# A four-layer graph network on one core: the beginning rewritten, half-block places split, the end taken by quarters

## The chip, the cores and the metric

The kernel runs on one core of a Trainium2 chip. TensorE (PE) multiplies and transposes, VectorE (DVE) and ScalarE (ACT) do the element-wise work, GpSimd (POOL) takes a little of it, and SyncE (SP) issues nearly all transfers between DRAM and the on-chip memory. The metric is the device time of one execution in microseconds (us); the time of the kernel before is the median of three runs, 4793.08 us (4787.59 to 4794.63).

## The reference, cut to what matters

Eight graphs (batches) of 2048 nodes with 128 features share one 0/1 adjacency matrix of 2048 x 2048. Four layers follow each other, each of the form `x = x + layer(relu(layernorm(x)))`:

```python
def layer0(x):                       # graph attention, one head
    x = x * node_weights[None, :, None] + node_bias[None, :, None] + x
    h = layernorm(x @ W) * ln_gamma + ln_beta
    s1, s2 = h @ a1, h @ a2
    e = leaky_relu(s1[:, :, None] + s2[:, None, :], 0.2)
    att = softmax(where(adj > 0, e, NEG_INF))
    return elu(att @ h + h)
def layer1(x):                       # attention with 4 heads of 32
    scores = where(adj == 0, -inf, q @ k.T / sqrt(32))
    return softmax(scores) @ v @ W_o + b_o
def layer2(x):                       # mean over the neighbours
    agg = (mask @ x) / maximum(deg, 1.0)
    return relu(x @ W_self + b_self + agg @ W_neigh + b_neigh)
def layer3(x):                       # graph attention, one head, no norm inside
    h = x @ W.T
    e = leaky_relu(s[:, :, None] + d[:, None, :], 0.2)
    return softmax(where(adj == 0, -1e9, e)) @ h
```

## The kernel before

**Units.** A row tile is 128 nodes (16 of them, `T`), a quarter is four row tiles (512 nodes, `G` = 4 quarters). Layers 0 and 3 work in six groups of destination tiles, `GROUPS`: four of three tiles and two of two (`n` = 3 or 2).

**Masks.** At the start each of the 16 row tiles of `adj` is loaded (1 MB, L1144) and turned into 0/1 in bf16 (`nb01`, VectorE, L1146). ScalarE makes of it an int8 mask (`pmt`, L1149; stored to DRAM as `pm_all`, L1152; the sum of the row is the degree's source). PE transposes the tile in 16 pieces into two PSUM tiles (`pmask`, L1162); VectorE copies the first (L1165), ScalarE the second (L1167) into `mst`, an fp8 mask, stored per group as `mg_all` (L1169). From that the fp8 tiles of layer 2, `mt_all`, are copied in DRAM (L1206, `regroup`). `degrees` makes the reciprocal degrees.

**Layers 0 and 3** (`gat_loop`). `layer0_ahead` makes layer 0's input: `weigh`, `scale` and `shift` on POOL (L592, L618, L621), two norms, transposes (`ptr`, L379), products (`ph`, L393). The node scores of one side are laid along the free dimension of all partitions by way of DRAM: `along_free` (row, `rowd`, broadcast load). `gat_rows` does that for all nodes (`s2b`, 1 MB); `gat_maximum` (L445) finds for one destination tile the greatest score among its neighbours with one VectorE pass over 128x2048; the maxima and scores of a group go the same way into `ab`. Then, for each of eight steps of a group, two source tiles at a time: `leaky` (ScalarE, L508), `lowered` (subtract the maximum, VectorE, L514), `exps` (ScalarE, L518), `masked` (VectorE, L523), `product` (PE, L534, into `gacc`), each stage one step behind the former; `finish` writes the result.

**Layer 1.** `before_attention` makes `q`, `k` and `v` of a batch, quarter by quarter, stores them and loads them back in the layouts that attention reads. The attention itself is 256 blocks (batch, 256 destination rows, head), each of 12 sub-steps: two halves (128 rows each) of six. In a half-block PE makes `sc` (S, L932), VectorE masks it and takes its maximum (`ttr`, L948, two of 128x1024, maxima in `amh`, `amn`), ScalarE takes exponentials (`exp`, L956), and PE transposes the result of a block before in two tiles `pt` (T0, T1, L968), which ScalarE copies to `eT` (C0, C1, L973), for the products with the values (V, `acc`, L983). Before: T0 at sub-step 3, T1 and C0 at 4, C1 at 5. At the end of a block's pair of heads `finished` transposes and normalises (`po`, `aoT`), and `back` multiplies with W_o (`pwo`, L1041) and adds to `x` (L1046); its functions are called one per sub-step from `pending`.

**Layer 2.** `layer2` makes the input (`pre2`: norm, `hm` in two bf16 parts, `h2T`), then for each quarter of destinations the sum over neighbours (`agg`: 48 matmuls `pagg`, L787, on `mt` tiles that `fetch` loads), scales it (`agT`, L805) and combines (`pn`, `y`).

**PSUM.** `psum(...)` gives one of three buffers. Results in it are read late: `later(f)` queues the reader, `settle` runs all of them, and `psum` runs the oldest when no buffer is free.

**The order.** Under `manual_schedule` the written order of PE, ScalarE, VectorE and POOL instructions is the order of their queues; SP's transfers are placed by the framework. The program is written in three stretches. First, `run(rest)`: ten masks merged with layer 0's input of batch 0, its row, its loop with six more masks, `before_attention(0)`. Second, the main periods, one for each batch: `work(side, end)` calls attention's sub-steps (`mains`) and after each a share of the side work by weights (layers 2 and 3 of the batch before, layer 0 of the next); `locked` puts one loop step per three sub-steps, each function of it into one of three cells by `PLACES` (or `PLACES_B` in the second half of a half-block), so that it stands at a fixed place among attention's instructions. In the last period the side work is layers 2 and 3 of batch 6. Third, the tail: `pre2`, `agg` with `pre3` partly between, and `loop3` of batch 7.

Of the kernel before, what the change touches and what calls it, by code (L numbers as in the profile page):

```python
# [31 lines left out]
def gnn_kernel(  # L32
# [167 lines left out]
    wq = load_w("wq", W_q)  # L200
    wk = load_w("wk", W_k)
    wv = load_w("wv", W_v)
    wo = load_w("wo", W_o)
    wself = load_w("wself", W_self)
    wneigh = load_w("wneigh", W_neigh)
    w3 = load_w("w3", W3)
    gam = load_row("gam", ln_g)
    bet = load_row("bet", ln_b)
    bo1 = load_row("bo1", b_o)
    bself = load_row("bself", b_self)  # L210
    bneigh = load_row("bneigh", b_neigh)

    nc.vector.tensor_scalar(bo1, bo1, -1.0, None, ALU.add)
# [28 lines left out]
    ones = const.tile([P, P], F32, name="ones")  # L242
# [5 lines left out]
    w0T = const.tile([P, P], F32, name="w0T")  # L248
# [7 lines left out]
    pw3 = psum("pw3", (P, P))  # L256
    nc.tensor.transpose(pw3, w3, ident)
    nc.vector.tensor_copy(w3T[:, 0:P], pw3)

    pwa = psum("pwa", (P, 2))  # L260
    nc.tensor.matmul(pwa, w3, a12_3, start=True, stop=True)
    nc.vector.tensor_copy(w3T[:, P : P + 2], pwa)
# [133 lines left out]
    def along_free(col, dst, n):  # L396
# [5 lines left out]
        for g in range(4):  # L402
            nc.sync.dma_start(
                out=d[0:n, g * 32 : (g + 1) * 32], in_=row[g * 32 : g * 32 + n, :]
            )
# [27 lines left out]
    def gat_rows(st):  # L433

        st["s2b"] = new(sp2, "s2b", "s2b", (P, N))
        along_free(st["s2n"], st["s2b"], T)
# [12 lines left out]
    def gat_loop(st, finish, maxima, gap):  # L449
# [15 lines left out]
        def maximum(k, q):  # L465
            i0, n = GROUPS[k]
            if maxima and q < n:
                gat_maximum(st, i0 + q)
# [4 lines left out]
        def shifts(k):  # L473
# [3 lines left out]
            nc.vector.tensor_tensor(u, s1, st["mn"][:, i0 : i0 + n], ALU.subtract)  # L477
# [5 lines left out]
        def spread(k):  # L483
            n = GROUPS[k][1]
            t = new(abp, "ab", "ab", (P, 2 * n * P))
            along_free(gr[k]["cab"], t, 2 * n)
# [94 lines left out]
    def layer0_ahead(b):  # L581
# [3 lines left out]
        def load(g):  # L585
            h[g] = new(hp3, "h", "h", (P, 4, P))
            nc.sync.dma_start(out=h[g], in_=x_chunk(b, g))

        def weigh(g):
            for k in range(4):  # L590
                t = 4 * g + k
                nc.gpsimd.tensor_scalar(  # L592
# [24 lines left out]
        def scale(g):  # L617
            nc.gpsimd.tensor_tensor(hv(g), hv(g), bc_mid(gam, 4), ALU.mult)  # L618

        def shift(g):  # L620
            nc.gpsimd.tensor_tensor(hv(g), hv(g), bc_mid(bet, 4), ALU.add)  # L621
# [52 lines left out]
    attn, ready = {}, {}  # L674

    def before_attention(b):
# [34 lines left out]
        def project_v(g):  # L711
# [16 lines left out]
        steps = Steps()  # L728
        steps.skewed(
            G,  # L730
            norm_stages(lambda g: xb[g], hdst) + [turned, project, project_v],
            1.0,
        )
        return steps

    def layer2(b):
# [26 lines left out]
        def rest1(g):  # L763
# [6 lines left out]
        steps = Steps()  # L770
        steps.skewed(
            G,
            norm_stages(lambda g: xb[g], hdst) + [part0, rest0, part1, rest1],
            4.0,
        )
# [63 lines left out]
        return steps, agg  # L839

    def layer3(b, gap=1):
# [13 lines left out]
        def project(g):  # L855
            if g == 0:
                st["haug"] = new(bp, "big", "haug", (P, T, P + 1))
# [9 lines left out]
        pre = Steps()  # L867
        pre.skewed(
            G,
            norm_stages(lambda g: xb[g], hdst)  # L870
            + [turned, project],
            1.0,
        )
        pre.add(0.5, settle)
        pre.add(1.0, lambda: gat_rows(st))
# [16 lines left out]
        return pre, gat_loop(st, finish, True, gap)  # L892
# [99 lines left out]
    def finished(blk):  # L992
# [45 lines left out]
        def back():  # L1038
# [7 lines left out]
            ao["last"] = later(lambda: nc.vector.tensor_tensor(xg, pw, xg, ALU.add))  # L1046
# [12 lines left out]
    SUB = 12  # L1059
    state = {"exp": None, "old": None, "older": None, "ahead": None, "pair": None, "ao": None}  # L1060

    def block_steps(n):
# [36 lines left out]

        def sub(t, s):  # L1100
            def go():
                if t == 0 and s == 0:
                    begin()
                old, older = state["old"], state["older"]
                if s == 0 and n < len(blocks):
# [294 lines left out]
```

## Time and profile before

| What | Value |
|---|---|
| median of 3 runs | 4793.08 us (4787.59 to 4794.63) |
| the profiled execution | 4792.7 us |
| its span | 4790.8 us |
| instructions | 87729 |
| mean granted TensorE clock | 0.943 |
| PE, DVE, ACT, POOL busy | 4126.7, 3906.3, 3613.4, 454.9 us |
| first mask (`nb01`) starts | 14.3 us |
| first step of layer 0's loop | 117.7 us |
| first exponential of attention | 296.9 us |
| last attention update of `x` | 4572.2 us |

The page cuts the span into 40 slices of 119.8 us; a digit is the busy share of a slice in tenths. Stages can be asked for by windows. A line of the timeline gives start, length, engine, line of the kernel, operation, written and read tile with shapes, and in brackets the engine's idle time before it and what ended it. Busy times are of one profiled execution; the time of that execution is the span and 1.9 us around it.

### The profile page before, as it was taken

How to read it: one execution, taken by the hardware profiler on the slowest of the kernel's cores; microseconds unless marked ns; L12 is line 12 of the kernel's file. 1: busy time of each engine (PE TensorE's matmuls, PEld its weight loads, DVE VectorE, ACT ScalarE, POOL GpSimd, SP SyncE). 2: the span in 40 equal slices, each digit the busy share in tenths (PEclk: the TensorE clock that was granted, in tenths of full speed). 3: DMA queues.
4: the chain of work that ended last, by engine and by line, in shares of the span. 5: the costliest groups of instructions: out<-in, count | busy, mean ns of one | idle time of the engine just before them, and what ended most of it. 6: DMA issues, size and time to landing. Idle time of an engine off the chain costs nothing.

```text
span 4790.8 us, 87729 instructions
## 1 busy us (share of the span) xinstructions
PE 4126.7 (86%) x33290; PEld 2842.0 (59%) x33290; DVE 3906.3 (82%) x8337; ACT 3613.4 (75%) x5121; POOL 454.9 (9%) x413
## 2 busy tenths in 40 slices
PE   2569998998898988998799988989889998989976
PEld 2535665576656666575665766567665666646645
DVE  5967777888978898788988889788987898658849
ACT  4637986698868988598885978689885988749926
POOL 2020002001200031001300012000310000000000
PEclk7768999999999999999999999999999999999988
DMA  8432113323232232412233132322324123222122
GB/s 268 137 91 57 46 40 114 95 59 102 79 123 62 68 103 76 133 51 86 82 103 102 59 101 77 120 66 68 103 74 134 50 73 99 79 77 61 52 89 76
DMA packets 308354, 423.34 MB, mean 88 GB/s; under 512 B 61222, under 2 KB 177628, under 8 KB 303836
## 3 DMA queue, kind: packets, MB, share of 16 engines
q1 hardware_dynamic: 305984, 416.85, 28.7%
q8 instruction: 263, 4.31, 0.4%
q14 instruction: 159, 1.30, 0.1%
q10 hardware_dynamic: 1948, 0.87, 0.1%
HBM read 365.78 MB, written 55.98 MB: 88 GB/s over the span
## 4 chain that ended last, share of the span: by engine, by line
PE 33%; DVE 29%; ACT 28%; issue 6%; DMA 3%; SPq 1%; ACTq 0%; DVEq 0%
ACT e L956 8%; ACT eT L973 8%; PE pt L968 7%; DVE e L948 7%; PE pagg L787 7%; PE gacc L534 6%; ACT ge L508 6%; PE sc L932 5%; DVE dump L445 4%; DVE ge L514 4%; DVE ge L523 4%; PE acc L983 3%; ACT ge L518 3%; PE ph L393 1%; DVE ln_s L336 1%
## 5 line engine op out<-in xcount | busy, mean ns | idle before, releaser
L973 ACT COPY eT<-pt 128x1024 f32<-128x1024 f32 x1024 | 1007.3, 1012 | 568.7 <-PE pt L968 566.0
L948 DVE CUSTOM_DVE_ANT_0 e<-sc,pm 128x1024 f32<-128x1024 f32 x1024 | 1211.5, 1220 | 212.0 <-PE sc L932 207.0
L534 PE MATMUL gacc<-haug,ge 128*128 128x129 f32 x8192 | 1122.4, 288 | 178.3 <-DVE ge L523 94.6
L968 PE MATMUL pt<-ident,e 128*128 128x128 f32 x8192 | 1079.0, 282 | 159.0 <-DVE amh L948 74.1
L534 PEld LDWEIGHTS gacc<-haug,ge 128*128 128x128 f32 x8192 | 1016.7, 199 | 335.5 <-issue 264.8
L968 PEld LDWEIGHTS pt<-ident,e 128*128 128x128 f32 x8192 | 943.5, 145 | 285.1 <-DVE amh L948 101.7
L956 ACT ACTIVATE e<-e,amn 128x2048 f32<-128x2048 f32 x512 | 1031.4, 2014 | 29.6 <-DVE amn L952 29.6
L508 ACT ACTIVATE ge<-ab,s 128x384 f32<-128x384 f32 (+1 forms) x1536 | 803.5, 577 | 121.5 <-DMA ab<-rowd 74.0
L932 PE MATMUL sc<-ks,qr 32*128 32x512 f32 x4096 | 786.9, 660 | 71.5 <-ACT eT L973 46.2
L514 DVE TENSOR_TENSOR ge<-ge,ab 128x768 f32<-128x768 f32 (+1 forms) x768 | 683.8, 890 | 52.5 <-ACT ge L508 46.2
L523 DVE SCALAR_TENSOR_TENSOR ge<-mg,ge 128x768 f32<-128x768 fp8e4 (+1 forms) x768 | 666.6, 868 | 24.7 <-ACT ge L518 23.2
L518 ACT ACTIVATE ge<-ge 128x768 f32<-128x768 f32 (+1 forms) x768 | 595.1, 776 | 118.0 <-DVE ge L514 115.9
L445 DVE CUSTOM_DVE_ANT_0 dump<-s2b,pmg 128x2048 bf16<-128x2048 f32 x256 | 585.5, 2287 | 39.4 <-DMA s2b<-rowd 32.2
L983 PE MATMUL acc<-eT,vv 128*32 128x256 f32 x8192 | 587.6, 397 | 2.6 <-ACT eT L973 2.6
L346 POOL TENSOR_TENSOR ln_r<-ln_ve,neg_half 128x4 f32<-128x4 f32 x160 | 207.2, 1295 | 3868.4 <-DVE ln_ve L340 3623.7
L983 PEld LDWEIGHTS acc<-eT,vv 128*32 128x32 f32 x8192 | 206.8, 111 | 508.7 <-issue 428.0
L932 PEld LDWEIGHTS sc<-ks,qr 32*128 32x128 f32 x4096 | 241.6, 189 | 263.9 <-ACT eT L973 142.5
L787 PE MATMUL pagg<-mt,hm 128*128 128x512 fp8e4 x1536 | 356.1, 381 | 9.3 <-DVE agT L805 9.3
L787 PEld LDWEIGHTS <-hm 128*128 128x128 bf16 x1536 | 147.2, 98 | 183.6 <-issue 30.7
L379 PE MATMUL ptr<-ident,h 128*128 128x128 f32 x512 | 92.3, 307 | 54.2 <-DVE amh L948 19.3
L1036 DVE TENSOR_TENSOR aoT<-po,rT 128x256 f32<-128x256 f32 x64 | 27.1, 424 | 127.6 <-ACT rT L1031 127.5
L379 PEld LDWEIGHTS ptr<-ident,h 128*128 128x128 f32 x512 | 66.8, 155 | 85.5 <-issue 28.8
(126 smaller groups left out, 2601.8 us busy)
## 6 DMA issues: line engine op xcount, KB each, us to landing
pmg<-pm_all SPq DMA_DIRECT2D x256, 256.0 KB
mg<-mg_all SPq DMA_DIRECT2D x128, 384.0 KB
pm<-pm_all SPq DMA_DIRECT2D x128, 256.0 KB
qr<-qd SPq DMA_DIRECT2D x1024, 32.0 KB
mt<-mt_all SPq DMA_DIRECT2D x64, 512.0 KB
ab<-rowd SPq DMA_DIRECT2D x64, 384.0 KB
adj<-in_adj_dram SPq DMA_DIRECT2D x16, 1024.0 KB
s2b<-rowd SPq DMA_DIRECT2D x16, 1024.0 KB
```

The costliest lines, as they stand in the source:

```text
L445: nc.vector.tensor_tensor_reduce(dump, st["s2b"], pm, UP, HIGHEST, ALU.add, ALU.min, st["mn"][:, it : it + 1])
L508: nc.scalar.activation(e[:, c, :], gr[k]["s1"], AF.Prelu, bias=st["s2"][:, j : j + 1], alpha=ALPHA)
L514: nc.vector.tensor_tensor(e, e, bc_mid(gr[k]["m"], 2), ALU.subtract)
L523: nc.vector.scalar_tensor_tensor(e, mt, BIG, e, ALU.mult, ALU.min)
L534: nc.tensor.matmul(gr[k]["acc"][:, q, :], e[:, c, q * P : (q + 1) * P], st["haug"][:, j, :], start=(j == 0 and q == 0), stop=(j == T - 1), ...
L787: nc.tensor.matmul(st["pa"], st["hm"][:, j, s, :], st["mt", g, j // 8][:, j % 8, :], start=(j == 0 and s == 0), stop=(j == T - 1 and s == ...
L932: nc.tensor.matmul(blk["sc"][g // 2][:, (g % 2) * 512 : (g % 2 + 1) * 512], blk["q"][r, t * P : (t + 1) * P], ks_t[b, hh][r, :], start=Tru ...
L948: nc.vector.tensor_tensor_reduce(e[:, c], blk["sc"][h], pm[:, c], UP, HIGHEST, ALU.add, ALU.min, mh[:, h : h + 1])
L956: nc.scalar.activation(blk["e"][t], blk["e"][t], AF.Exp, scale=-1.0, bias=blk["mn"][:, t : t + 1], accum_out=blk["ao"]["sum"][:, t, blk["h ...
L968: nc.tensor.transpose(pt[:, c, t, :], blk["e"][t][:, j * P : (j + 1) * P], ident)
L973: nc.scalar.copy(eT, blk.pop(("pt", w)).rearrange("p c t n -> p c (t n)"))
L983: nc.tensor.matmul(pair["acc"][g * HD : (g + 1) * HD, blk["hh"] % 2, :], vv_t[blk["b"], blk["hh"]][:, j, :], blk["eT"][w][:, g, :], start= ...
```

## The change

**The beginning.** Ten constants that layer 0 doesn't need are loaded from SP after the first inputs, and what is derived from them is made later. The inputs `h` and four tiles of `adj` are loaded ahead. `weigh`, `scale` and `shift` of batch 0 run on VectorE. `nb01` comes from a pool of two buffers, all 16 transposes of a mask go to one PSUM tile that ScalarE copies alone, and a mask's work is in three skewed stages. Eleven masks are merged with layer 0's input; the other five stand before or in the first steps of the loop. Three of the four quarters of `before_attention(0)` are put into layer 0's loop, after the groups that end them.

**Half-blocks.** Places are counted in six sub-steps, given by `ORDER`: T0 and T1 both at 3, C0 at 4, C1 at 5. `locked` has six cells for a loop step, of which every second is preceded by a sub-step; the side work's share is 0.55 for 0.6.

**The end.** In the last main period, after layer 3 of batch 6, stand layer 2's input of three quarters of batch 7 and the first seven entries of `agg` (one load, six gathers: 36 matmuls). In the tail layer 3's input is written by quarters between the gathers, the row `s2b` in two halves, and the maxima by halves of 1024 (32 instead of 16); the first halves stand among the gathers. The mask tiles for them are loaded four at a time.

```diff
-    w3 = load_w("w3", W3)
...
-    nc.vector.tensor_scalar(bo1, bo1, -1.0, None, ALU.add)
+    late = [("wq", W_q), ("wk", W_k), ("wv", W_v), ("wo", W_o), ("wself", W_self)]
...
+    def load_late():
+        for t, ap in late.values():
+            nc.sync.dma_start(out=t, in_=ap if len(ap.shape) == 2 else ap.partition_broadcast(P))
...
-                gat_maximum(st, i0 + q)
+                if "halves" in st:
+                    st["halves"][2](1, i0 + q)
+                else:
+                    gat_maximum(st, i0 + q)
...
-            nc.vector.tensor_tensor(u, s1, st["mn"][:, i0 : i0 + n], ALU.subtract)
+            if "halves" in st:
+                mnh = st["mnh"][:, :, i0 : i0 + n]
+                nc.vector.tensor_tensor(u, mnh[:, 0, :], mnh[:, 1, :], ALU.min)
+                nc.vector.tensor_tensor(u, s1, u, ALU.subtract)
+            else:
+                nc.vector.tensor_tensor(u, s1, st["mn"][:, i0 : i0 + n], ALU.subtract)
...
-    def layer0_ahead(b):
+    def layer0_ahead(b, eng=nc.gpsimd):
...
-            nc.gpsimd.tensor_tensor(hv(g), hv(g), bc_mid(gam, 4), ALU.mult)
+            eng.tensor_tensor(hv(g), hv(g), bc_mid(gam, 4), ALU.mult)
...
+        def some(gs):
+            steps = Steps()
+            steps.skewed(
+                len(gs),
+                [
+                    lambda i, f=f: f(gs[i])
+                    for f in norm_stages(lambda g: xb[g], hdst) + [turned, project, project_v]
+                ],
+                1.0,
+            )
...
+        def masks_of(k):
+            t = st["pm", k] = new(ep, "e", "pmh", (P, 4, N), I8)
+            for i in range(4):
+                nc.sync.dma_start(out=t[:, i, :], in_=pm_all[4 * k + i])
+        def rows(half):
+            if half == 0:
+                st["s2b"] = new(sp2, "s2b", "s2b", (P, N))
+                st["mnh"] = small("mnh", (P, 2, T))
+            c = slice(half * 1024, (half + 1) * 1024)
+            along_free(st["s2n"], st["s2b"][:, c], 8 * half, 8)
+        def maximum(half, it):
+            c = slice(half * 1024, (half + 1) * 1024)
+            dump = new(op, "dump", "dump", (P, 1024), BF16)
+            nc.vector.tensor_tensor_reduce(
+                dump, st["s2b"][:, c], st["pm", it // 4][:, it % 4, c], UP, HIGHEST, ALU.add,
+                ALU.min, st["mnh"][:, half, it : it + 1],
+            )
+        stages = norm_stages(lambda g: xb[g], hdst) + [turned, project]
+        if last:
+            st["halves"] = (masks_of, rows, maximum)
+            pre = [Steps([(1.0, [lambda f=f, g=g: f(g)]) for f in stages]) for g in range(G)]
+        else:
+            pre = Steps()
+            pre.skewed(G, stages, 1.0)
+            pre.add(0.5, settle)
+            pre.add(1.0, lambda: gat_rows(st))
...
+            def add():
+                nc.vector.tensor_tensor(xg, pw, xg, ALU.add)
+                summed.append((b, ib // 2))
+            ao["last"] = later(add)
...
+    ORDER = [
+        ["S", "V0", "exp"],
+        ["V1"],
+        ["ttr"],
+        ["T0", "T1"],
+        ["C0"],
+        ["C1"],
+    ]
...
                     begin()
+                for name in ORDER[s]:
+                    part(t, name)
                 old, older = state["old"], state["older"]
-                if s == 0 and n < len(blocks):
-                    scores(blk, t)
...
-                if s in (3, 4) and real("old"):
-                    turned(old, 2 * t + s - 3)
-                if s in (4, 5) and real("old"):
-                    copied(old, 2 * t + s - 4)
...
+        nb01[it] = new(tp, "eT", "nb01", (P, N), BF16)
+        nc.vector.tensor_scalar(nb01[it], adj_t.pop(it), 0.0, None, ALU.is_gt)
+        load_adj(it + 4)
...
+        pt = psum("pmask", (P, T, P), BF16)
+        for jt in range(T):
+            nc.tensor.transpose(pt[:, jt, :], nb01[it][:, jt * P : (jt + 1) * P], ident_bf)
+        later(lambda: nc.scalar.copy(mst[gk][:, :, c : c + P], pt, saturate=False))
...
-        def one(it):
...
-                if g == 0:
-                    nc.vector.tensor_copy(dst, pt, saturate=False)
-                else:
-                    nc.scalar.copy(dst, pt, saturate=False)
...
+        steps.skewed(T, [neighbours, turned_raised, mask_stored], 5.0)
...
-        st0, pre = layer0_ahead(0)
...
+        st0, pre = layer0_ahead(0, nc.vector)
+        for g in range(G):
+            st0["load"](g)
+        for it in range(4):
+            load_adj(it)
+        load_late()
         xs[0] = []
-        load_x(0)
         masks_all = mask_steps()
-        early, late = Steps(masks_all[:10]), Steps(masks_all[10:])
-        rest = merged(early, pre)
-        rest.add(1.0, lambda: gat_rows(st0))
-        rest.extend(merged(layer0_loop(0, st0, True), late, 0.35))
-        rest.extend(before_attention(0))
+        n = 11
+        rest = merged(pre, Steps(masks_all[:n]))
+        rest.add(1.0, lambda: gat_rows(st0), lambda: load_x(0))
+        rest.add(1.0, late_constants)
         run(rest)
+        xb0 = xs[0]
+        loop = layer0_loop(0, st0, True)
+        quarters, queue, others = before_attention(0), [], masks_all[n:]
+        start = len(loop) - 9 * len(GROUPS) - 6
+        for _ in range(3):
+            run([others.pop(0)])
+        n_late = len(others)
+        for k, step in enumerate(loop):
+            run([step])
+            if others and (k + 1) * n_late >= 0.1 * len(loop) * (n_late - len(others)):
+                run([others.pop(0)])
+            for g, group in enumerate((1, 2, 3, 5)):
+                if k == start + 9 * group + 13:
+                    queue.extend(quarters([g]))
+            if queue:
+                run([queue.pop(0)])
+        run(others + queue)
...
-        PLACES = {'product': 1, 'masked': 0, 'exps': 1, 'lowered': 0, 'leaky': 1, 'ended': 1, 'closed': 0, 'maxi': 0, 'other': 2}
-        PLACES_B = {'product': 1, 'masked': 0, 'exps': 0, 'lowered': 1, 'leaky': 0, 'ended': 1, 'closed': 1, 'maxi': 1, 'other': 2}
+        PLACES_A = {
+            "product": 5, "masked": 1, "exps": 3, "lowered": 1, "leaky": 3,
+            "ended": 1, "closed": 1, "maxi": 1, "other": 5,
+        }
+        PLACES_B = {
+            "product": 5, "masked": 1, "exps": 1, "lowered": 3, "leaky": 1,
+            "ended": 3, "closed": 3, "maxi": 0, "other": 5,
+        }
...
+                cell = [[] for _ in range(6)]
+                places = PLACES_B if pos[0] % 6 >= 3 else PLACES_A
...
-                    cell[(i * 3) // len(parts)].append(p)
-                for c in cell:
-                    mains[pos[0]]()
-                    pos[0] += 1
+                    cell[2 * ((i * 3) // len(parts)) + 1].append(p)
+                for i, c in enumerate(cell):
+                    if i % 2 == 1:
+                        mains[pos[0]]()
+                        pos[0] += 1
...
-                    locked(both[n:], tail, 0.6)
+                    locked(both[n:], tail, 0.55)
...
+                pre2, agg = layer2(B - 1)
+                side.extend(pre2(range(G - 1)))
+                side.extend(agg[:7])
...
+        pre3, loop3, (masks_of, rows, maximum) = layer3(B - 1, last=True)
+        beside = {}
+        def put(k, *fns):
+            beside.setdefault(k, []).append((1.0, list(fns)))
+        first = list(pre2([G - 1]))
+        for g in range(G - 1):
+            k = 9 * (g + 1) + 3
+            for i, (_, fns) in enumerate(pre3[g]):
+                put(k + 1 + i, *fns)
+            if g == 1:
+                put(k + 7, lambda: rows(0))
+        for k in range(4):
+            put(20 + 3 * k, lambda k=k: masks_of(k))
+        todo = [(lambda it=it: maximum(0, it)) for it in range(T)]
+        rest = Steps(first)
+        def some(n):
+            for _ in range(n):
+                if todo:
+                    rest.add(1.0, todo.pop(0))
+        for k in range(7, len(agg)):
+            rest.append(agg[k])
+            rest.extend(beside.pop(k, []))
+            if k >= 33:
+                some(1)
+        for k in sorted(beside):
+            rest.extend(beside[k])
+            some(1)
+        for _, fns in pre3[G - 1]:
+            rest.add(1.0, *fns)
+            some(1)
+        rest.add(1.0, settle)
+        rest.add(1.0, lambda: rows(1))
+        some(T)
+        run(rest + loop3)
```

## Prediction

> **What bounds the kernel now.** I read the page first (busy time, the slices, the chain), then the busy time by stage, then the order of events at both ends.
>
> ```profile
> PE 4126.7 (86%) x33290; PEld 2842.0 (59%) x33290; DVE 3906.3 (82%) x8337; ACT 3613.4 (75%) x5121; POOL 454.9 (9%) x413
> PE   2569998998898988998799988989889998989976
> ...
> DVE  5967777888978898788988889788987898658849
> ...
> PE 33%; DVE 29%; ACT 28%; issue 6%; DMA 3%; SPq 1%; ACTq 0%; DVEq 0%
> ```
>
> Three engines share the chain, so no single one is the bound. But the first two slices of PE (119.8 us each) stand at 2 and 5, and the last two at 7 and 6: the ends are slack on PE, the middle is not. By stage (columns: stretch, length, busy PE, PEld, DVE, ACT, POOL, granted clock, DMA share, GB/s):
>
> ```profile
> 0.00:120.00 120.00, 30.66 (x249) 26.57 (x249) 64.22 (x167) 49.07 (x66) 31.36 (x46) 0.77 0.81 268
> 120.00:240.00 120.00, 71.77 (x488) 66.47 (x489) 115.07 (x190) 79.25 (x131) 0.00 (x0) 0.79 0.43 137
> 2670.00:2710.00 40.00, 38.73 (x352) 29.84 (x352) 34.21 (x67) 37.90 (x57) 0.00 (x0) 1.00 0.18 51
> 2940.00:2980.00 40.00, 34.65 (x282) 25.71 (x280) 38.90 (x72) 29.93 (x43) 6.80 (x4) 0.90 0.26 74
> 4560.00:4680.00 120.00, 76.33 (x412) 45.10 (x410) 49.38 (x158) 20.56 (x35) 8.50 (x9) 0.78 0.30 95
> 4680.00:4791.00 111.00, 73.94 (x512) 69.66 (x512) 105.00 (x158) 76.71 (x137) 0.00 (x0) 0.85 0.25 77
> ```
>
> Until 120 us no engine is busy for more than 54%: chains and DMA (0.81) set the pace. From 120 to 240 and from 4680 on, VectorE does (115 of 120, 105 of 111). The middle changes between PE (38.73 of 40) and VectorE (38.90 of 40). From 4560 to 4680 again nobody is full. The events that mark the ends (start, length, instruction, in brackets the idle time before it and what ended it):
>
> ```profile
> 97.34 2.29 DVE L445 CUSTOM_DVE_ANT_0 dump<-s2b,pmg 128x2048 bf16<-128x2048 f32 x1 [10.24 <-DMA s2b<-rowd]
> 117.66 2.13 ACT L508 ACTIVATE ge<-ab,s 128x384 f32<-128x384 f32 x4 [5.12 <-DMA ab<-rowd]
> 287.23 1.23 DVE L948 CUSTOM_DVE_ANT_0 e<-sc,pm 128x1024 f32<-128x1024 f32 x1 [11.78 <-PE sc L932]
> 4572.15 0.42 DVE L1046 TENSOR_TENSOR x<-pwo,x 128x256 f32<-128x256 f32 x1 [0.80 <-PE pwo L1041]
> 4634.73 0.69 DVE L805 TENSOR_TENSOR agT<-pagg,dv 128x512 f32<-128x512 f32 x1 [4.07 <-PE pagg L787]
> 4660.33 2.29 DVE L445 CUSTOM_DVE_ANT_0 dump<-s2b,pmg 128x2048 bf16<-128x2048 f32 x1 [7.41 <-DMA s2b<-rowd]
> ```
>
> So: first leaky of layer 0 at 117.7, x ready at 258.5, attention from 287; after the last attention update (4572.2) come layer 2's gathers to 4634.7, layer 3's input, its row in DMA until 4660.3, and its loop.
>
> **Part 1, the beginning.** (a) *Masks.* Each loses VectorE's cast `mst` (1.23) and gets one ScalarE copy of 128x2048. That form is not in the trace; 128x512 takes 0.58 and 128x1024 1.01, so 1.01 + 2 × 0.43 = 1.87. With `pmt` (1.94 from start to next start) a mask costs ScalarE 3.8. All 16 now stand before the loop: 61, plus layer 0's own 16 × 0.41 + 4 × 0.6 + 4 × 0.59 = 11, from about 16 us on: ScalarE is free at 88. VectorE has 16 × 1.22 of `nb01` and less than that again; the second `nb01` buffer hides PE's 16 transposes (1.07 to 1.89) behind ScalarE. The skewed order puts the last `nb01` before the third maximum; that comes near 82, the row of `cab` near 86, and from it to the first leaky the trace has 6.5 (end) to 9.4 (beginning): 94, taken as 95 against 117.7: **−22.7**.
>
> DMA may not allow that. Some 29 MB (adj 16, masks out 8, rows, maxima's masks, x) must move before it. The 268 GB/s at a share of 0.81 make 331 when full, so 88 us: just enough; at the 268 itself, 108, and −10. Against the change speaks a rule of the Trainium skill ("DMA: Bandwidth & Descriptors", Issuing engines are not separate DMA queues): all issuers end on the same 16 engines, so ten constants (0.65 MB) moved from ScalarE's queue to SP's win no bandwidth, only order. By it I book nothing for that move; its row (19 issues on ScalarE before its first work) would have given 2 or 3 us.
>
> (b) *POOL.* Scaling and shifting of layer 0's input go to VectorE. The trace has one POOL operation at 65.33 and a VectorE one at 65.56, which takes 0.17 at 59.12:
>
> ```profile
> 65.33 1.18 POOL L618 TENSOR_TENSOR haug<-haug,gam 128x512 f32<-128x512 f32 x1 [2.25 <-ACT mst L1167]
> 65.56 0.97 DVE L425 TENSOR_TENSOR ln_z<-ln_z,ln_r 128x8 f32<-128x8 f32 x1
> 59.12 0.17 DVE L425 TENSOR_TENSOR ln_z<-ln_z,ln_r 128x8 f32<-128x8 f32 x1
> ```
>
> The skill ("SBUF — State Buffer", Who interferes with whom) says that a VectorE operation with two inputs in SBUF and a reading POOL operation lock each other out for a whole instruction. By the rule all 31 us of POOL could stand against VectorE; by the row some 8 operations lost 0.8 each, 7 in all, about what 8 × 0.69 + 16 × 0.34 = 11 cost VectorE anew. I take the row: nothing, as VectorE has 45% idle there.
>
> (c) *Loop.* 117.7 to 258.5 is 140.8, VectorE-bound. Four masks leave it (4 × 2.45 = 9.8) and the degrees (5.5); three quarters of `before_attention` enter (2.5 each): 133: **−7.8**. (d) *After it* came four quarters, 258.5 to the first full scores at 285.2. One remains: statistics 1.4, power 1.0, apply 1.1, transposes 1.2, copy 0.6, projection 2.1, two copies 1.2, and 5.7 through DRAM as before: 14.3: **−12.4**. The early loads of the next input save its wait of 2.73 (row at 293.86): **−3**. Part 1: **−46**, between −33 (DMA) and −57.
>
> **Part 2, the 512 half-blocks.** Six half-places for three, both transposes together ahead of the copies, `pwo` behind both. Compared engine by engine, ScalarE's and VectorE's written orders hardly differ; PE's `po`, `pwo` and the gathers move past one transpose group. Counts stay. What can be gained is PE's wait for `pwo` (12.8 on `amh`, 6.9 on `eT`); two fifths of it, **−8**. What can be lost: both transposed tiles taken from PSUM at once, half as much again as PE's waits on `eT` (43.6 in 11 times), +20. Queued behind such a wait on PE are `po`, the side work's gathers and the next scores, for which VectorE's masking then waits.
>
> **Part 3, the last period.** Three of four quarters of layer 2's input move into it, with 36 of 192 gathers. Moved work: VectorE 11.6, ScalarE 5.5, PE 12 × 0.14. In 4440 to 4560 PE and ScalarE are busy for 112.9 and 112.4 of 120, so ScalarE's 5.5 are paid: **+5** (2 to 15). The gathers stand behind the last `pwo`; the hole from 4572 to the first gather hides them (uncovered, 36 × 0.2165 = 7.8):
>
> ```profile
> 4583.26 6.99 PE L787 MATMUL pagg<-mt,hm 128*128 128x512 fp8e4 x24
> ```
>
> **Part 4, the tail.** 24 gathers took 6.99, 0.29 each, later 0.2165. After the change 36 × 0.2165 run from 4572.2 to 4580, beside the last quarter's norm (5 us); its transposes 0.7; then 156 × 0.2165 = 33.8, four pauses of 2.6 less one, 7.7, and layer 3's transposes and projections of three quarters, 1.5 each: 4627 for 4634.7: **−8** (at 0.29, −4). Layer 3's input is then one quarter, 14.3 from `agT` to the row's transpose by its rows, where four took 18.0: **−3.7**. The row still takes 7.4; three maxima of 2.37 become three halves of 1.30, less 0.2 for the new minimum: **−3**. In the loop 13 maxima are halved, 13 × 1.07 less six small operations, and VectorE bounds it: **−12.5**. The first halves (16 × 1.30 = 21) lie in VectorE's idle time (49 of 120 busy); uncovered they would cost 21. Their masks are 16 loads of 256 KB on SP, queued among the gathers' own loads: 4 MB at a DMA share of 0.30, hidden; late, they would hold back VectorE's queue, and with it layer 3's last quarter. Part 4: **−27** (−18 to −36).
>
> Sum: −46 − 8 + 5 − 27 = −76 on the profiled execution's 4792.7 (span 4790.8, 1.9 around it), 0.4 below the median: **4717**.
>
> **Rivals.** *DMA and ScalarE keep pacing the beginning* (0.13): the leaky comes no earlier, since all masks precede it; the gains in (c) and (d) stay. For it: 0.81 DMA share, and 256-byte rows in the last two mask stores. Against: between 20 and 60 us 245 to 395 GB/s were moved. 4717 + 22.7 = 4740. *The tail's work comes back* (0.12): the last period pays VectorE's 11.6 and ScalarE's 5.5 in full, and cold PE, +15 for +5, tail −18: 4736. *PSUM binds the middle* (0.10, the other side): with both transposed tiles out, side matmuls wait for the first copy. For it: single waits on `eT` up to 7.3 us. Against: the copies were already PE's releaser, the later transpose now starts only one place earlier. The sum is spent at 84/512 = 0.16 per half-block; at 0.2 it is 102: 4717 + 8 + 102 = 4827. *The middle does not change at all*, since the orders are the same: 4725, inside the likeliest.
>
> **How the numbers follow.** Likeliest, 0.62: 4717, its own range 4690 to 4745. The first two rivals lie within 4730 to 4760; 0.03 for an unnamed larger gain. The PSUM case splits: 0.02 same, 0.08 slower, left outside. Range 4680 to 4760. Faster by over 0.2% (9.6 us, about what this kernel's measurement can tell from no change) 0.90, same 0.02, slower 0.08.
>
> **What would show it.** First leaky at 95 (over 108: DMA), x at 228, first full scores at 242, first `agT` wait gone, the last `agT` 55 after the last attention update, the loop of layer 3 at 103.5 long; the attention's half-blocks at the same 8.3 mean. It is wrong if half-blocks grow by 0.16, if first-half maxima delay layer 3's last quarter on VectorE, or if the last period grows by over 15.

## The result, and the profile after

The changed kernel takes 4715.71 us (median of 4 runs, 4711.7 to 4720.64) against 4793.85 us before (4 runs): a ratio of 0.984, with a 95% interval of 0.9823 to 0.9857. The forecast was 4717, between 4680 and 4760. The sum came out within 2 us, and none of its four terms did: that it came so near was luck. The profiled execution shows it: its span is 4709.9, 80.9 less than before.

The page of the changed kernel (busy time; slices of PE and VectorE; the chain by engine):

```profile
PE 4116.3 (87%) x33290; PEld 2845.2 (60%) x33290; DVE 3879.8 (82%) x8384; ACT 3619.7 (77%) x5121; POOL 471.4 (10%) x389
PE   3769998998899989999899988999889998989976
...
DVE  5967767888978888788988889788887899758758
...
PE 32%; DVE 32%; ACT 24%; issue 6%; DMA 5%; SPq 1%; POOL 0%; ACTq 0%; DVEq 0%; POOLq 0%
```

The first three slices of PE go from 2, 5, 6 to 3, 7, 6, and the last two still stand at 7 and 6. DMA's share of the chain rises from 3% to 5%. By stage (columns as before: stretch, length, busy PE, PEld, DVE, ACT, POOL, clock, DMA share, GB/s):

```profile
0.00:120.00 120.00, 39.23 (x320) 34.12 (x321) 71.30 (x214) 77.29 (x84) 13.21 (x22) 0.67 0.85 296
120.00:240.00 120.00, 86.04 (x530) 77.87 (x530) 115.96 (x214) 82.28 (x151) 23.33 (x6) 0.79 0.56 152
4560.00:4680.00 120.00, 69.26 (x457) 61.42 (x455) 106.35 (x199) 62.58 (x104) 2.85 (x2) 0.77 0.21 63
```

The events that answer to those shown of before (start, length, instruction, idle time before it and what ended it):

```profile
90.01 2.29 DVE L445 CUSTOM_DVE_ANT_0 dump<-s2b,pmg 128x2048 bf16<-128x2048 f32 x1 [14.56 <-DMA pmg<-pm_all]
110.27 2.13 ACT L516 ACTIVATE ge<-ab,s 128x384 f32<-128x384 f32 x4 [9.32 <-DMA ab<-rowd]
257.40 1.23 DVE L996 CUSTOM_DVE_ANT_0 e<-sc,pm 128x1024 f32<-128x1024 f32 x1 [6.82 <-PE sc L980]
4512.11 7.93 PE L814 MATMUL pagg<-mt,hm 128*128 128x512 fp8e4 x36
4512.31 0.42 DVE L1096 TENSOR_TENSOR x<-pwo,x 128x256 f32<-128x256 f32 x1 [0.21 <-PE pwo L1089]
4572.14 0.68 DVE L832 TENSOR_TENSOR agT<-pagg,dv 128x512 f32<-128x512 f32 x1
4605.64 2.13 ACT L516 ACTIVATE ge<-ab,s 128x384 f32<-128x384 f32 x4 [19.62 <-DMA ab<-rowd]
```

The first leaky came 7.4 earlier, where 22.7 were forecast. Behind the 110th microsecond more was won than forecast: the last attention update came 59.8 earlier, for 49. In the stretch from 4560 VectorE is at 106 of 120, where it had been at 49: layer 3's loop begins earlier. To see where the gain lies I took from each trace the starts of the 512 attention exponentials. Each half-block has one, a batch has 64; a period below runs from the sixth half-block of a batch to the sixth of the next, since the side work changes there:

| Stretch | before | after | difference | forecast |
|---|---|---|---|---|
| start to the first exponential | 296.9 | 267.2 | −29.6 | −46 |
| first period (69 half-blocks) | 498.3 | 491.2 | −7.2 | −1 |
| periods of batches 1 to 6 | 3334.0 | 3310.8 | −23.3 | −6 |
| last period to its last exponential | 428.3 | 428.9 | +0.5 | +4 |
| from there to the end | 233.3 | 211.9 | −21.4 | −27 |

(The −8 forecast for 512 half-blocks is spread over the three periods' rows by their length.) So the beginning and the end brought 22 us less than I said, the half-blocks in the periods up to batch 6 some 23 more.

### The profile page after: what moved, and what is told of

Read it like the earlier page. It is cut to its first block, busy times and chain, and to the rows that moved or that the text cites. A ratio compares the mean times of both kernels' runs of the same rounds, so it can differ in the third digit from the quotient of the medians.

```text
span 4709.9 us, 87689 instructions
## 1 busy us (share of the span) xinstructions
PE 4116.3 (87%) x33290; PEld 2845.2 (60%) x33290; DVE 3879.8 (82%) x8384; ACT 3619.7 (77%) x5121; POOL 471.4 (10%) x389
## 4 chain that ended last, share of the span: by engine, by line
PE 32%; DVE 32%; ACT 24%; issue 6%; DMA 5%; SPq 1%; POOL 0%; ACTq 0%; DVEq 0%; POOLq 0%
DVE e L996 9%; ACT e L1004 7%; ACT eT L1021 7%; PE gacc L542 7%; PE pt L1016 7%; PE pagg L814 6%; PE sc L980 5%; DVE dump L445 4%; DVE ge L522 4%; ACT ge L516 4%; DVE ge L531 4%; PE acc L1031 3%; ACT ge L526 2%; DMA ab<-rowd 2%; DVE ln_s L336 2%
## 5 line engine op out<-in xcount | busy, mean ns | idle before, releaser
L1016 PE MATMUL pt<-ident,e 128*128 128x128 f32 x8192 | 1066.5, 282 | 191.6 <-DVE amh L996 155.0
L980 PE MATMUL sc<-ks,qr 32*128 32x512 f32 x4096 | 773.2, 660 | 62.1 <-ACT eT L1021 44.6
L522 DVE TENSOR_TENSOR ge<-ge,ab 128x768 f32<-128x768 f32 (+1 forms) x768 | 667.9, 870 | 45.9 <-ACT ge L516 41.6
L531 DVE SCALAR_TENSOR_TENSOR ge<-mg,ge 128x768 f32<-128x768 fp8e4 (+1 forms) x768 | 666.4, 868 | 28.3 <-ACT ge L526 27.6
L346 POOL TENSOR_TENSOR ln_r<-ln_ve,neg_half 128x4 f32<-128x4 f32 x160 | 219.5, 1372 | 3863.5 <-DVE ln_ve L340 3615.9
L445 DVE CUSTOM_DVE_ANT_0 dump<-s2b,pmg 128x2048 bf16<-128x2048 f32 x240 | 549.2, 2288 | 40.5 <-DMA pmg<-pm_all 25.6
L1047 ACT COPY oT<-acc 128x512 f32<-128x512 f32 x128 | 74.8, 584 | 78.9 <-PE acc L1031 78.9
```

Of the source, the lines that this page charges most:

```text
L445: nc.vector.tensor_tensor_reduce(dump, st["s2b"], pm, UP, HIGHEST, ALU.add, ALU.min, st["mn"][:, it : it + 1])
L522: nc.vector.tensor_tensor(e, e, bc_mid(gr[k]["m"], 2), ALU.subtract)
L531: nc.vector.scalar_tensor_tensor(e, mt, BIG, e, ALU.mult, ALU.min)
L980: nc.tensor.matmul(blk["sc"][g // 2][:, (g % 2) * 512 : (g % 2 + 1) * 512], blk["q"][r, t * P : (t + 1) * P], ks_t[b, hh][r, :], start=Tru ...
L1016: nc.tensor.transpose(pt[:, c, t, :], blk["e"][t][:, j * P : (j + 1) * P], ident)
```

## The experiments

In each case the ratio is that of the timed runs against the kernel before on the same chip, with its 95% interval; parts of the trace are read from the profiled execution.

**One part alone** (e1 to e3). The parts of the diff were applied one at a time to the kernel before.

e1, only the beginning:

```diff
+        st0, pre = layer0_ahead(0, nc.vector)
+        n = 11
+        rest = merged(pre, Steps(masks_all[:n]))
...
```

> Only the new beginning (constants, masks, layer 0's input on VectorE, quarters in the loop); half-blocks and end as before. Prediction's part 1: -46, 4747. By the trace of the changed kernel the first exponential comes 29.6 us earlier: if nothing is given back in the periods, -30, 4763. If the first period's further 8 us also come from the beginning (regroup, later constants), -38, 4755.

Measured: 4759.05, ratio 0.9939 (0.9921 to 0.9957). The first exponential comes 31.6 earlier, the last one 36.9. The beginning gives 31 (timed runs) to 37 (trace), not 46, and the periods take nothing of it back.

e2, only the half-blocks:

```diff
+    ORDER = [["S", "V0", "exp"], ["V1"], ["ttr"], ["T0", "T1"], ["C0"], ["C1"]]
...
+                cell = [[] for _ in range(6)]
...
+                    locked(both[n:], tail, 0.55)
```

> Only the half-blocks (six half-places, order T0 T1 C0 C1, share 0.55); beginning and end as before. Prediction's part 2: -8, 4785. Rival theory from the changed kernel's trace (attention ends 30 us earlier relative to its own start): the middle carries the -27 to -30, 4764. Third: it gives nothing by itself, 4793, and the gain of the periods came from the beginning and the last period.

Measured: 4742.05, ratio 0.9902 (0.9886 to 0.9918). That is −48 alone, more than any theory said and the largest of the three. Periods 1 to 6 take 3298.7 (−35.3) and the last one 420.6 (−7.7); some 11 of the 35 are TensorE's granted clock, as is seen under e5.

e3, only the end:

```diff
+                pre2, agg = layer2(B - 1)
+                side.extend(pre2(range(G - 1)))
+                side.extend(agg[:7])
...
+        pre3, loop3, (masks_of, rows, maximum) = layer3(B - 1, last=True)
```

> Only the new end (last period and tail; two small constants share a buffer, which it needs for space); beginning and half-blocks as before. Prediction's parts 3 and 4: +5 and -27, 4771. By the trace of the changed kernel the stretch behind the last attention update is 21 us shorter, and the last period costs nothing: 4772. If the moved work is paid in full in the last period (rival), -10, 4783.

Measured: 4782.68, ratio 0.9983 (0.9976 to 0.9991). The profiled execution (span 4773.1) has the stretch behind the last exponential 21.6 shorter, as in the changed kernel, and the last exponential 3.9 later. That execution was among the fastest of 20; their median is only 7 to 8 below before. Where the others lose the rest is not seen here. The three alone add up to −31 − 48 − 7 = −86 against the −78 of all together.

**What in the half-blocks gains** (e4, e7, e9). e4 takes the transposes apart in the changed kernel:

```diff
-        ["T0", "T1"],
-        ["C0"],
+        ["T0"],
+        ["T1", "C0"],
```

> The changed kernel with the transposes apart again: T0 at sub-step 3, T1 and C0 at 4; half-places and share stay. If putting the transposes together is what shortens the periods, it falls back by 25 to 30, to 4743; if the half-places or the share do it, it stays at 4716 within 5; if the two together cost PSUM waits that the places make up, it is faster than 4716.

Measured: 4737.29, ratio 0.989 (0.9872 to 0.9909), 5 thousandths above the changed kernel: 24 us. Periods 1 to 6 take 3329.0 again, all but 5 of before's 3334.0. Single half-blocks show what is at work, since they repeat in every period: number 19 of a period (counted from 0) takes 9.63 in e4 (9.64 before) and 8.24 in the changed kernel. Here is the place in the timeline of e4, PE's and ScalarE's lines that matter, in order of time:

```profile
2058.60 1.04 PE L1016 MATMUL pt<-ident,e 128*128 128x128 f32 x8
2060.44 0.58 ACT L382 ACTIVATE h3T<-ptr 128x512 f32<-128x512 f32 x1
2060.91 1.00 ACT L1021 COPY eT<-pt 128x1024 f32<-128x1024 f32 x1
2061.07 1.16 PE L393 MATMUL ph<-w3T,h3T 128*128 128x130 f32 x8 [1.43 <-ACT h3T L382]
2062.06 1.04 PE L1016 MATMUL pt<-ident,e 128*128 128x128 f32 x8
2063.19 1.01 ACT L1021 COPY eT<-pt 128x1024 f32<-128x1024 f32 x1 [1.28 <-PE pt L1016]
```

and the same place of the changed kernel:

```profile
2050.86 1.91 PE L1016 MATMUL pt<-ident,e 128*128 128x128 f32 x16
2052.67 0.59 ACT L382 ACTIVATE h3T<-ptr 128x512 f32<-128x512 f32 x1
2053.15 1.93 ACT L1021 COPY eT<-pt 128x1024 f32<-128x1024 f32 x2
2053.32 1.16 PE L393 MATMUL ph<-w3T,h3T 128*128 128x130 f32 x8 [0.54 <-ACT h3T L382]
```

In e4 a side product (`ph`, layer 3's input) stands between the two transposes and waits 1.43 for its operand. T1 is queued behind it, ScalarE then waits 1.28 for T1, and the next exponential stands behind ScalarE's copy. With the transposes together the product waits behind both, for 0.54, and hides the rest of its wait behind T1.

e7 keeps the transposes together and puts the three old places and the share 0.6 back:

```diff
-        PLACES_A = {
-            "product": 5, "masked": 1, "exps": 3, "lowered": 1, "leaky": 3,
-            "ended": 1, "closed": 1, "maxi": 1, "other": 5,
...
+        PLACES = {'product': 1, 'masked': 0, 'exps': 1, 'lowered': 0, 'leaky': 1, 'ended': 1, 'closed': 0, 'maxi': 0, 'other': 2}
...
-                    locked(both[n:], tail, 0.55)
+                    locked(both[n:], tail, 0.6)
```

> The changed kernel with the three old places and the share 0.6, transposes together. If the transposes together carry the whole gain of the middle: 4716 within 5. If the half-places carry a part: slower by that part, 4725 to 4735.

Measured: 4750.94, ratio 0.9918 (0.9897 to 0.9938): the places and the share are worth 37 us to the changed kernel, and the theory that the transposes carry everything falls. With the old places, putting the transposes together gives nothing that the runs show: the beginning and the end alone (e1 and e3, multiplied) make 0.992. Periods 1 to 6 take 3350.9 in the trace, 17 more than before; but that execution was the slowest of the four (4763.15), and the granted clock accounts for more than the 17 (see e5). So in the traces' periods neither of the two helps by itself, and both together do. In the timed runs e4 lies some 15 us below that 0.992, of which its trace shows 5 in periods 1 to 6.

e9 changes the share alone:

```diff
-                    locked(both[n:], tail, 0.55)
+                    locked(both[n:], tail, 0.6)
```

> The changed kernel with the side work's share at 0.6 again; half-places and transposes stay. The old places and 0.6 together cost 6 us in each of six periods, 5 of them in half-blocks 37 to 51. If the share carries that, these half-blocks take 168 us again for 163.7, and the time is 4741 to 4747; if the half-places do it, 4716 within 5.

Measured: 4704.11, ratio 0.9825 (0.981 to 0.984): about 7 below the changed kernel, which the intervals do not tell from nothing. Half-blocks 37 to 51 take 159.7 instead of 163.7 (168.8 in e7). e9 and e7 have the same share and the same transposes and differ in the places, by some 45 us: it is the half-places that e7 lacked, not the share. What they do is seen in PE's waits over five periods, those of batches 1 to 5 (who waits for whom: us in all, times, longest), before:

```profile
PE pt L968 <- DVE amh L948: 50.7, 58, 2.4
PE gacc L534 <- DVE x L881: 49.1, 18, 5.7
PE pt L968 <- ACT eT L973: 36.7, 5, 7.3
PE gacc L534 <- DVE hp L658: 22.6, 20, 2.3
PE ph L393 <- ACT h3T L382: 15.1, 15, 1.4
```

in the changed kernel:

```profile
PE pt L1016 <- DVE amh L996: 126.5, 66, 5.6
PE gacc L542 <- DVE x L929: 15.6, 5, 3.1
PE gacc L542 <- DVE hp L669: 12.0, 10, 2.3
PE ph L393 <- ACT h3T L382: 6.6, 10, 0.8
```

and in e7, with the old places:

```profile
PE pt L1016 <- DVE amh L996: 87.0, 48, 4.7
PE gacc L542 <- DVE x L929: 52.4, 15, 5.7
PE pt L1016 <- ACT eT L1021: 28.6, 5, 5.7
PE gacc L542 <- DVE hp L669: 19.8, 20, 2.3
PE ph L393 <- ACT h3T L382: 6.6, 10, 0.8
```

`gacc` has one buffer. The first product of a group waits until VectorE has read the former group's sum (`hp`, `x`), and behind it wait PE's transposes. The new places put the product one sub-step later in both halves of a half-block, a group's end one sub-step earlier in the first half, and VectorE's maxima earlier in the second (no run takes these three apart): 71.7 falls to 27.6. In e4 and e9, with the new places, these two rows are 27.4 and 26.9; in e7, with the old ones, 72.2. So the wait on `gacc` follows the places. The product's wait for `h3T` follows the transposes: 15.1 before, 14.2 in e4, 6.6 in the changed kernel and in e7. From before to the changed kernel 89 us of waits went (44 on `gacc`, 37 of `pt` on `eT`, 8 on `h3T`), and 76 came back as PE's wait for VectorE's maxima (`amh`), which is what is late next; all of PE's waits together went from 279.0 to 263.6, and the stretch is 18.9 shorter. The 37 on `eT` are no gain of the places: in e9, which has them and the share 0.6, this wait is 30.6 and the one for `amh` 96.9, together 127.5 beside the 126.5 of the changed kernel.

**An empty step** (e5). In combination the half-blocks brought 12 less in periods 1 to 6 than in e2 (3310.8 for 3298.7). The end's part of the diff gives layer 2's input one more stage for all batches, an assertion without instructions. It makes eleven weighted steps of ten:

```diff
-                    for f in [begin]
+                    for f in ([begin] if b + 1 == B else [])
```

> The changed kernel, with layer 2's new first stage (an assertion that issues nothing) only where batch 7 needs it, so that the side work of the periods is spread over ten steps of layer 2's input again instead of eleven. Theory: that empty step shifts the gathers against attention and costs the periods some 2 us each (half-blocks 5 to 8 of a period take 60.6 us in the changed kernel and 60.3 with the half-blocks alone, but the whole period 556.2 and 554.0): 12 faster than the changed kernel, 4703. Rival: the difference lies in the share of the end and of chance, 4716 within 4.

Measured: 4714.51, ratio 0.9838 (0.982 to 0.9855): nothing in the time. In the trace periods 1 to 6 take 7.9 less (3302.9), as the theory had it for the most part, but the last period takes 438.9 instead of 428.9. Neither is shown to be the step's doing. Three more runs with the changed kernel's order in these periods (e6, e8, e10) take 3306.5 to 3315.1 in periods 1 to 6, and e11 (below), with its order in the last period, takes 435.1 there. What differs is the clock granted to TensorE, which in these traces is 1.0 or 0.5, mostly in spells of 3.4 us or a multiple of it. The same product of layer 3's input in the last period, with the row of its stretch (columns as before), first in the changed kernel, then in e5:

```profile
4175.31 1.16 PE L393 MATMUL ph<-w3T,h3T 128*128 128x130 f32 x8
4173.00:4190.00 17.00, 14.01 (x108) 8.89 (x111) 11.12 (x49) 8.08 (x13) 2.55 (x4) 1.00 0.01 1
4173.90 2.10 PE L393 MATMUL ph<-w3T,h3T 128*128 128x130 f32 x8 [0.69 <-ACT h3T L382]
4170.00:4187.00 17.00, 13.85 (x63) 8.86 (x61) 8.70 (x50) 5.75 (x8) 3.10 (x4) 0.50 0.07 17
```

At half clock eight matmuls take 2.10 instead of 1.16. In the last period PE was busy at half clock for 39.6 us in e5 and for 15.3 in the changed kernel. If half of such time is the price (an estimate from 2.10 and 1.16), the clock accounts for 12 us, and e5's last period is not longer otherwise. With that half taken off, the last period is 419 to 422 in all eleven traces with the new end, which measured 428.6 to 438.9. Periods 1 to 6, for which PE's time at half clock is 171.7 before, 175.2 in the changed kernel, 150.1 in e2, 157.6 in e5 and 218.8 in e7, then fall into two groups: 3221 to 3231 in the nine traces that have the new places and the transposes together, 3241 to 3248 in the five that lack one or both (before, e1, e3, e4, e7). So the gain of the two together stands without the clock, at some 20 us from group to group, and the differences of e2, e5 and e7 from their groups are the clock's. Whether the order decides where the clock is halved is not shown: with one order (changed kernel, e6, e8, e10) PE's time at half clock in these periods is 152 to 175.

**The beginning** (e6, e8). e6 moves 2 MB of transfers behind the first loads of the loop:

```diff
-        rest.add(1.0, lambda: gat_rows(st0), lambda: load_x(0))
+        rest.add(1.0, lambda: gat_rows(st0))
...
+        last = others.pop()
...
+            if k == 13:
+                load_x(0)
+                run([last])
```

(`last` makes the degrees and stores the bias rows.)

> The changed kernel, with 2 MB of transfers (x of batch 0 and layer 2's bias rows with the degrees) moved behind the first loads of the loop. If DMA sets the beginning: 1 MB less ahead of the first maximum and 2 MB less ahead of the first leaky, at 300 GB/s 6 to 7 us: leaky at 104 for 110.3, time 4709. If ScalarE's sixteen masks set it: leaky stays at 110 within 1, time 4716.

```profile
104.77 2.13 ACT L516 ACTIVATE ge<-ab,s 128x384 f32<-128x384 f32 x4 [6.68 <-DMA ab<-rowd]
```

The leaky comes at 104.77, 5.5 earlier, as expected if DMA sets it. Yet the time is 4712.13, ratio 0.9833 (0.9817 to 0.9849), and the first exponential does not come earlier at all (268.5 for 267.2). The degrees' work on VectorE, 5.5 by the prediction's row, had lain in the idle time ahead of the leaky. Moved, it lies in the loop, which VectorE fills (115.96 of 120): the loop from the first leaky to the last update of x takes 141.2 instead of 135.1. So DMA sets the leaky, and a gain there has to be had without uncovering the degrees.

e8 puts the scaling of layer 0's input back on POOL:

```diff
-        st0, pre = layer0_ahead(0, nc.vector)
+        st0, pre = layer0_ahead(0)
```

> The changed kernel with weigh, scale and shift of batch 0 on POOL again. Prediction's step (b): nothing, 4716 within 3. If POOL holds VectorE up for its whole busy time (some 18 us more of it before 120 us) and the beginning waits for VectorE: first leaky later by 5 to 10, 4721 to 4726. If DMA sets the beginning, nothing of either is seen.

Measured: 4717.35, ratio 0.9845 (0.9827 to 0.9864): no difference from the changed kernel. The first leaky comes at 114.2, 3.9 later, and the first exponential 3.0 later; the first period is 3.4 shorter in this execution, in which PE was busy at half clock for 59.5 us of it instead of 72.3 (worth 6 by the estimate under e5).

**The end** (e10). The sixteen first-half maxima all stand behind the second row's issue:

```diff
-            if k >= 33:
-                some(1)
...
         rest.add(1.0, lambda: rows(1))
         some(T)
```

> The changed kernel with the sixteen first-half maxima all behind the second row's issue instead of among the gathers and layer 3's last quarter. Prediction: uncovered they cost 21, and the row's flight of 7 covers a part: 14 slower, 4730. If VectorE has too little idle time among the gathers anyway (the first-half maxima of the changed kernel end at 4595, when the second row lands), some 5 to 9 slower, 4721 to 4725. If they hold VectorE's queue up for layer 3's last quarter, faster than 4716.

```profile
4572.75 0.68 DVE L832 TENSOR_TENSOR agT<-pagg,dv 128x512 f32<-128x512 f32 x1
4584.90 0.21 DVE L400 STREAM_TRANSPOSE row<-s2n 128x32 f32<-128x32 f32 x1
4609.65 0.21 DVE L400 STREAM_TRANSPOSE row<-cab 128x32 f32<-128x32 f32 x1
4615.63 2.13 ACT L516 ACTIVATE ge<-ab,s 128x384 f32<-128x384 f32 x4 [31.16 <-DMA ab<-rowd]
```

Measured: 4722.13, ratio 0.986 (0.9847 to 0.9874), about 9 slower (the intervals overlap; in the trace the stretch behind the last exponential is 8.3 longer). Without maxima in VectorE's queue the last quarter is 3.2 faster (12.15 from `agT` to the row for 15.33), and the maxima behind it cost 12.6 more (24.75 to the row of `cab` for 12.10). So both theories hold in part: the cover is worth 12.6, and 3.2 of it are paid by the chain that they stand in.

**Versions that the experiments point to** (e11, e12). e11 loads x of batch 0 behind the first row `ab`, leaving the degrees where they are, and keeps the empty stage for batches 6 and 7 only:

```diff
-                    for f in [begin]
+                    for f in ([begin] if b + 2 >= B else [])
...
+            if k == 13:
+                load_x(0)
```

> The changed kernel with two edits: x of batch 0 (1 MB) is loaded behind the first row ab, and layer 2's empty first stage stands only for batches 6 and 7. By the experiments: the row comes 3 earlier and the degrees' VectorE work stays in its shadow, -3; the six periods take 8 less as without the empty stage, and the last period stays at 429 as with it: 4705. If the last period depends on how the periods before it end, it varies by up to 10: 4700 to 4715.

Measured: 4705.75, ratio 0.9822 (0.9809 to 0.9836), about 8 below the changed kernel, with overlapping intervals. The first exponential is 2.9 earlier, periods 1 to 6 take 3303.6 (−7.2), the last one 435.1; by the estimate under e5 these 6 more, and most of the 7 less, are the clock's.

e12 is e11 with the share of e9:

```diff
-                    locked(both[n:], tail, 0.55)
+                    locked(both[n:], tail, 0.6)
```

> The changed kernel with all that the experiments point to: x of batch 0 behind the first row ab, layer 2's empty first stage for batches 6 and 7 only, share 0.6. With the share alone half-blocks 37 to 51 took 159.7 for 163.7 in five periods, 5 more in the sixth: -10 on the changed kernel; with the other two edits -9. If they add, 4697; if the last period shifts as it did with the empty stage gone (+6 to +10), 4700 to 4707.

Measured: 4693.28 (5 runs, 4685.82 to 4696.79), ratio 0.9796 (0.9782 to 0.981): faster than both kernels, about 21 below the changed one. Periods 1 to 6 take 3287.6 (−23.2) and the last one 428.7. The gain in the periods is not one of waits: over five of them PE waits 264.9 (263.6 in the changed kernel). PE was busy at half clock for 133.3 in periods 1 to 6 instead of 175.2, worth 21 by the estimate. That e12's order brings the higher clock is likely, since all five runs are faster than any of the changed kernel's, but with one trace it is not shown.

## Why the prediction was right, and where it was not

The time was right because two errors, 22 us in the beginning and the end and some 23 in the half-blocks, happened to stand against each other: luck, not a sum that held. Point by point:

**Part 1, (a) masks: the size was wrong.** ScalarE's cost of a mask was right: the copy of 128x2048, estimated at 1.87 from two smaller ones, took 1.85 to 1.87. What failed is the DMA term, "some 29 MB ... must move before it". By 95 us 29.38 MB had moved, but others than the needed ones; before the leaky at 110 it was 32.87 MB, at 299 GB/s (share 0.85), where I had taken 331 for a full queue. My list has one load of x where there are two (`h` and `x`, 1 MB each), and lacks the constants, the loop's own masks and the bias rows. Small requests came late too: the first maximum's mask, 256 KB, was issued at 80.70 and let VectorE go on at 90.01. So the beginning, at −30, missed its own range of −33 to −57. My rival "DMA and ScalarE keep pacing the beginning" described this place, with 4740 as its price; the part that it put on ScalarE wasn't needed. Of the rule that I weighed (the Trainium skill, "DMA: Bandwidth & Descriptors", Issuing engines are not separate DMA queues) no run tests the issuer alone; e6 shows that the bytes ahead of the row count. **(b) POOL**: nothing, as I took it (e8); the rule of mutual exclusion ("SBUF — State Buffer", Who interferes with whom) has at most the 3.9 by which the leaky was later to show for itself. **(c) Loop**: 135.1 for 133. **(d)** From the last update of x to the first exponential 38.4 became 21.9, −16.5 for −15.4.

**Part 2 failed.** The step reads "What can be gained is PE's wait for `pwo`"; I took −8. Periods 0 to 6 gained 30, and the half-blocks alone 46. The profile's list of PE's waits had the rows that moved, `gacc` on `x` and `hp` (71.7 over five periods), and I passed them over: my list of what moves on PE names `po`, `pwo` and the gathers, but not the loop's `product`, which goes one sub-step later, and I had concluded that a change of a sub-step or less could not matter. It does where a matmul waits for a one-buffer result and others stand behind it in PE's queue. The rival on the other side, PSUM taken twice, did not appear as a loss: taking the transposes apart made the kernel slower, not faster (e4). PE's wait of `pt` on `eT` fell from 36.7 to nothing; it is 28.6 in e7 and 30.6 in e9, which have the share 0.6, and e9 is no slower.

**Part 3**: the last period stayed as it was (+0.5 for +5). Without the moved work it took 420.6 (e2), so the moved work costs 8.3 there, some 11 with the clock taken off as under e5, within the 2 to 15 given. What I had left out is that the half-blocks gain in this period too. The 36 gathers were hidden behind the last update, as the line at 4512.11 shows, at 0.22 each.

**Part 4**: −21 for −27. From the last update to the last `agT` 59.8 for 62.6: −2.8, not −8. A quarter of gathers now takes 15.3 (4540.39 − 4525.08) for 13.1 before. The term "1.5 each" for layer 3's pieces between the gathers was too low, at 2.2, because they also stand in VectorE's queue ahead of `agT`, for which PE then waits 1.67 instead of 0.78; the last quarter's `hm` came 1.3 late; and the last quarter took 16.5, with a first-half maximum right ahead of its `agT`. To the row −2.6 for −3.7 (e10 names the maxima in VectorE's queue), to `cab` −3.4 for −3, the loop 104.3 for 116.1, −11.8 for −12.5.

## What to carry to other kernels

When two sets of instructions are moved by half a place, list every wait that ends at an instruction of either and ask for each whether it starts or ends elsewhere; an unchanged order on two engines says nothing of the third. Work that lay hidden in the hole of a transfer is paid for when it is moved out together with the transfer (e6): move the transfer and leave the work, as e11 did. And before a few us in one stretch of one trace are given a cause, compare how long PE was busy at half clock in it: an empty step seemed to move the last period by 10, and it was the clock.

## What the runs showed of the hardware beyond that

The same half-block in five successive periods repeats within 0.01 us in more than half of the 64 places of the changed kernel (number 19: 9.63 in e4, 8.24 in the changed kernel), so 1 us at such a place is read from a trace although whole runs scatter by 10. And PE's busy time isn't a fixed cost of its instructions: for the same 20644 matmuls of five periods it is 2516.97 before and 2491.81 with the half-blocks alone, so of the 29.7 us gained there 25.2 are shown as busy time and only 3.5 as waits of PE. About half of the 25 is the granted clock: PE was busy at half clock for 153.8 of these us before and for 129.5 in e2, which is worth 12 by the estimate under e5. The other half stays unexplained.
